# A selective scan on one core: 5 of 16 products with C moved to GpSimd and summed by accumulating DMAs

## The chip, the core and the metric

The kernel runs on one core of one Trainium2 chip. The metric is the device time of one execution, in microseconds (us); shown is the median of several runs. TensorE (PE), VectorE (DVE), ScalarE (ACT), GpSimd (POOL) and the DMA queue of SyncE (SP) work side by side; an instruction waits for semaphores that others set. Within an engine the instructions run in the order in which the program holds them.

## The reference, cut to what matters

Four layers follow one another on 4 images of 128 channels and 64 x 64 points: layer 0 is softmax attention over the 4096 points, layer 1 two 3x3 convolutions with quantised weights, layer 2 a Mamba block with group norm, layer 3 a second attention. The change is in layer 2. With 256 inner channels, 16 states per channel and a length of 4096 it computes

```python
def step(h, inp):
    dt_t, B_t, C_t, x_t = inp
    dA = jnp.exp(dt_t[..., None] * A)
    dBx = dt_t[..., None] * B_t[:, None, :] * x_t[..., None]
    h = dA * h + dBx
    y = jnp.einsum('bdn,bn->bd', h, C_t)
    return (h, y)
...
y = _selective_scan(xh, dt, Bmat, Cmat, A, D)
y = y * jax.nn.silu(z)
return y @ W_out
...
x = jax.nn.silu(_group_norm(x, gn_gamma, gn_beta))
return x + x_hsi
```

The sum over the 16 states in `y` (the einsum) is what the change distributes anew.

## The kernel before

Layer 2 of an image is cut into 8 groups of 512 points, so that there are 32 groups g. In each group the 16 states n are worked through one by one; m = 16 g + n counts these 512 steps. A tile of a step is 128 x 2 x 512 floats: both halves of the 256 channels, 512 points. One step takes

- a fetch on SP (`fetches`, L996): the rows B and C of state n, broadcast to 128 partitions (512 KB) into one of three tiles `bc`. It waits until the product with C of step m-3 is done, which is the last reader of that tile;
- on ACT two exponentials `da` into PSUM (`decays`, L1009);
- on DVE a multiplication `hs = ud * B` (`scans`, L1036), the product with C of the step before (`readout`, L1026, `hs = hs * C`), and two scans, one for each half (L1044). The first input of a scan, `da`, lies in PSUM, and the second, `hs`, in SBUF. The multiplications L1036 and L1026 have both inputs in SBUF;
- on ACT a copy of the last column of `hs` (`lasts`, L1019), from which the next group of the image goes on. It must be made before `hs` is overwritten by the product;
- on POOL an addition `y = y + hs` (`additions`, L1061).

After the 16th addition of a group POOL multiplies y by silu(z) (L1065, the gate), PE multiplies by W_out (L923), ACT writes the result to a tile `yo` of its own, and DVE takes the statistics of the group norm (L936). When an image's 8 tiles are there, the norm, silu (L972) and the residual (L976) are made in place, and the 8 tiles go to DRAM (L987). Layer 3 reads them from there (L375, tile `x_in`). There are three tiles `hs` and eight tiles `yo`.

Layers 0 and 3 of all images are worked through in 8 stages: (0,0), (0,1), (0,2), (3,0), (0,3), (3,1), (3,2), (3,3), given as layer and image. A stage computes blocks of energies on PE (L494), exponentials on ACT (L513) and weighted sums on PE (L556 for layer 0, L565 for layer 3), and runs beside the scans of some image. Stage (3,b) starts when layer 2 of image b is in DRAM.

The order of all instructions on all engines is made when the kernel is built: each piece of work is a Python generator that yields `op(engine, time, *needs)`, and `Order.run` (L79) takes the piece that could start earliest, by times written in the code and a rank. It treats the SBUF port that DVE and POOL share as one resource: each operation of POOL, and each of DVE that is marked `port=True`, has it to itself. The hardware then runs this order with waits on semaphores.

Of the kernel before, what the change touches and what calls it, by code (L numbers as in the profile page):

```python
# [8 lines left out]
F32 = mybir.dt.float32  # L9
# [7 lines left out]
ALU = mybir.AluOpType  # L17
# [24 lines left out]
VP = P + 1  # L42

# [90 lines left out]
def conv_seq_kernel(ctx: ExitStack, tc: tile.TileContext, i: dict, out: bass.AP):  # L134
# [226 lines left out]

    def stage_input(s):

        layer, b = stages[s]
        for c in range(NTB // 2):
            need = [("x2", b, 2 * c), ("x2", b, 2 * c + 1)] if layer == 3 else []
            need += [("sums", s * NS - 2 + c // 2), ("exp", s * NS - 1, 1)]
            yield op("SP", 0.1, *need, lag=3.5)
            x = att.tile([P, 2, 2, CB], F32, tag="p", name="x_in", bufs=4)
            x = x.rearrange("p a b c -> p a (b c)")  # L370
            if layer == 0:
                src = i["x"][b].rearrange("c (k r) w -> c k (r w)", r=ROWS)[:, 2 * c : 2 * c + 2]
            else:
                src = x2s[b][2 * c : 2 * c + 2].rearrange("c p t -> p c t")
            nc.sync.dma_start(out=x, in_=src)  # L375
            staged[s, c] = x
            mark("in", s, c)

    def operands(s):
# [19 lines left out]
        def high_low(o, g, key, bias, low, n):  # L399

            c = len(lows)
            lows.append(("low", s, c))
            yield op("ACT", 0.2 + n * 1e-3, (*key, "in"), *lows[c - 1 : c])
            h = att.tile([P, 2 * TB], F32R, tag="h", name="h", bufs=1)
            nc.scalar.activation(h[:, 0:n], g, AF.Identity, bias=low[1], scale=low[0])
            yield op("DVE", 0.06 + n * 1.2e-3)
            nc.vector.scalar_tensor_tensor(o, g, bias, h[:, 0:n], ALU.add, ALU.subtract)
            mark(*key)
            mark(*lows[c])
# [3 lines left out]
        for c in range(NTB // 2):  # L413
            g, key = yield from to_bank(1.9, ("in", s, c))
            if c == 0:
                its[s] = it = att.tile([P, N], dt, tag="it", name="it", bufs=1)
# [10 lines left out]
            need = [("sums", s * NS - 1)] if c == 0 and s else []  # L427
            g, key = yield from to_bank(1.1 if layer == 0 else 2.6, *need)
            if c == 0:
                v = att.tile([P, NJ * VP], F32, tag="v", name="v", bufs=1)  # L430
                if layer == 0:
                    vts[s] = v.rearrange("p (a b) -> p a b", b=VP)
                    nc.gpsimd.memset(vts[s][:, :, P:VP], 1.0)
                    jts[s] = att.tile([P, NJ // 2 * P], dt, tag="j", name="j", bufs=1)
                else:
                    both = v[:, 0 : NJ * P].rearrange("p (a b) -> p a b", a=2)
                    jts[s] = both[:, 0]
                    vts[s] = both[:, 1].rearrange("p (a b) -> p a b", b=D3)
# [83 lines left out]
    def accumulations():  # L522
        for t in filter(added, range(len(stages) * NS)):
            k, q = divmod(t, NQ)
            for h in range(2):
                if q == 0 and h == 0:
                    continue
                need = [("exp", t, h)]
                if q == 0 and k:
                    need.append(("sums", t - 1))  # L530
                yield op("DVE", 1.25, *need, port=True)
                if q == 0:
                    accs[k] = att.tile([P, 2, 2, CB], F32, tag="acc", name="acc", bufs=1)
                other = ps[t, 0] if q == 0 else accs[k]
                nc.vector.tensor_add(accs[k], ps[t, h], other)  # L535
# [248 lines left out]
    stats, live, bcs, das, hss = {}, {}, {}, {}, {}  # L784
# [129 lines left out]
    def output():  # L914
        for g in range(NG):
# [4 lines left out]
            yo = big.tile([P, TB], F32, tag="yo", name="yo", bufs=NTB)  # L920
# [15 lines left out]
            nc.vector.bn_stats(stats[b][:, c, :], yo)  # L936
            if c < NTB - 1:
                continue

# [29 lines left out]
            x2 = [live.pop(("yo", NTB * b + k)) for k in range(NTB)]  # L969
            for k in range(NTB):  # L970
                yield op("ACT", 0.69, table="silu")
                nc.scalar.activation(x2[k], x2[k], AF.Silu, bias=sh, scale=rs)  # L972
                mark("silu", b, k)
            for k in range(NTB):
                yield op("DVE", 0.75, port=True)
                nc.vector.scalar_tensor_tensor(  # L976
                    x2[k],
                    x1s[b % 2][:, 1 + k * TB : 1 + (k + 1) * TB],
                    1.0 / LEVELS,
                    x2[k],  # L980
                    ALU.mult,
                    ALU.add,
                )
                if k == 0:
                    x2s[b] = dram.tile([NTB, P, TB], F32, tag="x2", name="x2_d")
                yield op("SP", 0.1, lag=2.5)
                nc.sync.dma_start(out=x2s[b][k], in_=x2[k])  # L987
                mark("x2", b, k)
# [40 lines left out]
    def scans():  # L1029
        for m in range(NM):  # L1030
            g, n = divmod(m, DS)
            need = [("add", m - 3)] if m > 2 else []
            yield op("DVE", 1.25, ("bc", m), ("ud", g), *need, port=True)
            ud = live["in", g][1]
            hss[m] = hs = pair("hs", "hs", 3)
# [3 lines left out]
            if m:  # L1039
# [16 lines left out]
    def additions():  # L1056
        for m in range(NM):
            g, n = divmod(m, DS)
            yield op("POOL", 2.36, ("c", m), ("y", g))
# [3 lines left out]
            if n == DS - 1:  # L1063
                yield op("POOL", 2.4, ("sz", g))
# [503 lines left out]
```

## Time and profile before

| what | value |
|---|---|
| median of 3 runs | 3625.69 us (3621.45 to 3629.59) |
| profiled execution: its own time | 3621.05 us |
| its span | 3618.9 us |
| DVE busy | 3037.0 us, 84% of the span |
| PE busy | 3130.2 us, 86% |
| ACT busy | 2522.3 us, 70% |
| POOL busy | 1320.5 us, 36% |
| DMA queue of SP | 34.2% of 16 engines' span |

The profiler takes one execution. The page gives each engine's busy time, and groups of instructions by line with busy time, the mean length of one and the idle time before them. Other views are the timeline (instructions in order of time), sums by stretches of the span, and the waits. A first stretch up to 234 us has no scans, and from 3273 us on none is left: there only stage (3,3) runs.

### The profile page before, as it was taken

To read this page: it belongs to the slowest core of one execution; us is meant where nothing else is said; L and a number is where in the kernel's file an instruction comes from. 1 tells how busy PE (TensorE), PEld (TensorE's weight loads), DVE (VectorE), ACT (ScalarE), POOL (GpSimd) and SP (SyncE) were. 2 spreads that over 40 slices of the span, in tenths; PEclk is the share of its full clock that TensorE was granted. 3 is DMA by queue.
4 is the path that set the end of the run, shared out by engine and by line. 5 is a ranking of instruction groups with operands and counts; after the bars stand their busy time and mean duration, and the time that the engine had idled before them with its cause. 6 is when DMAs were issued, how large, how long until landed. Compare 5 with 4: busy or idle time off the path is not lost.

```text
span 3618.9 us, 69982 instructions
## 1 busy us (share of the span) xinstructions
PE 3130.2 (86%) x29495; PEld 2256.7 (62%) x29495; DVE 3037.0 (84%) x2872; ACT 2522.3 (70%) x3721; POOL 1320.5 (36%) x571
## 2 busy tenths in 40 slices
PE   5999899998999998999899999989779999205999
PEld 3988688886888755555787775555435555003665
DVE  2059999999999599999999999999999999994333
ACT  3477788787778777777787777777667776534444
POOL 0014344443444134444443344444444444451000
PEclk8999999999999999999999999999889999557999
DMA  2023433343434334444333333444354444341000
GB/s 72 1 58 93 107 96 89 96 100 103 98 93 100 88 96 106 111 108 129 90 98 106 79 105 95 107 107 106 101 139 108 109 110 106 94 105 62 13 19 17
DMA packets 203652, 327.76 MB, mean 91 GB/s; under 512 B 50608, under 2 KB 53440, under 8 KB 203328
## 3 DMA queue, kind: packets, MB, share of 16 engines
q1 hardware_dynamic: 196384, 322.09, 34.2%
q8 instruction: 233, 3.82, 0.4%
q10 hardware_dynamic: 6944, 1.10, 0.2%
q14 instruction: 91, 0.75, 0.1%
HBM read 304.27 MB, written 18.87 MB: 89 GB/s over the span
## 4 chain that ended last, share of the span: by engine, by line
PE 47%; DVE 33%; ACT 9%; issue 7%; DMA 3%; ACTq 0%; POOL 0%; SPq 0%; DVEq 0%; POOLq 0%
DVE hs L1044 14%; PE us L556 13%; PE e L494 11%; PE us L565 8%; DVE hs L1036 7%; DVE hs L1026 5%; PE us L589 3%; PE conv L704 2%; ACT p L513 2%; ACT da L1009 2%; PE yo L923 2%; PE xh L793 1%; PE proj L420 1%; DMA bc<-bc_d 1%; PE proj L462 1%
## 5 line engine op out<-in xcount | busy, mean ns | idle before, releaser
L1061 POOL TENSOR_TENSOR y<-y,hs 128x1024 f32<-128x1024 f32 x512 | 1218.2, 2379 | 1913.8 <-DVE hs L1026 1856.7
L513 ACT ACTIVATE p<-e 128x1024 f32<-128x1024 f32 x1024 | 1005.4, 1018 | 320.4 <-PE e L494 298.8
L1044 DVE TENSOR_TENSOR_SCAN hs<-da,hlast,hs 128x512 f32<-128x512 f32 x896 | 1099.9, 1264 | 16.1 <-ACT da L1009 15.9
L556 PE MATMUL us<-v,p 128*128 128x129 f32 x8192 | 1016.0, 281 | 47.4 <-ACT p L513 41.0
L556 PEld LDWEIGHTS us<-v,p 128*128 128x128 f32 x8192 | 960.4, 194 | 100.1 <-ACT p L513 45.2
L1009 ACT ACTIVATE da<-dt,amat 128x512 f32<-128x512 f32 x1024 | 702.5, 691 | 289.7 <-DVE hs L1044 284.7
L1026 DVE TENSOR_TENSOR hs<-hs,bc 128x1024 f32<-128x1024 f32 x512 | 666.9, 1303 | 15.2 <-ACT hlast L1019 14.6
L1036 DVE TENSOR_TENSOR hs<-ud,bc 128x1024 f32<-128x1024 f32 x512 | 653.0, 1275 | 1.0 <-DMA bc<-bc_d 0.6
L565 PE MATMUL us<-p,v 128*32 128x256 f32 x8192 | 525.0, 387 | 39.5 <-ACT p L513 37.2
L494 PE MATMUL e<-it,v 64*128 64x256 f32 x4096 | 528.2, 398 | 18.9 <-ACT p L513 17.9
L494 PEld LDWEIGHTS e<-it,v 64*128 64x128 f32 x4096 | 382.2, 191 | 168.9 <-issue 96.3
L565 PEld LDWEIGHTS us<-p,v 128*32 128x32 f32 x8192 | 238.1, 110 | 269.4 <-issue 86.0
L589 PE MATMUL us<-p,ones 128*32 128x256 f32 x3328 | 219.8, 382 | 0.0
L494 PE MATMUL e<-it,j 64*128 64x256 f32 x2048 | 196.0, 309 | 19.0 <-ACT v L396 9.9
L494 PEld LDWEIGHTS e<-it,j 64*128 64x128 f32 x2048 | 140.7, 189 | 77.8 <-issue 28.1
L793 PEld LDWEIGHTS <-w 128*128 128x128 bf16 x576 | 53.2, 99 | 192.9 <-issue 152.5
L1019 ACT COPY hlast<-hs 128x2 f32<-128x2 f32 x448 | 85.1, 190 | 120.0 <-DVE hs L1044 115.0
L589 PEld LDWEIGHTS us<-p,ones 128*32 128x32 f32 x3328 | 102.8, 110 | 87.9 <-issue 27.0
L793 PE MATMUL z<-x,w 128*128 128x512 fp8e4 x192 | 54.7, 395 | 117.4 <-ACT sz L816 112.4
L1044 DVE TENSOR_TENSOR_SCAN hs<-da,hs 128x512 f32<-128x512 f32 x128 | 149.4, 1203 | 1.4 <-ACT da L1009 1.3
L923 PE MATMUL yo<-y,w_out 128*128 128x512 f32 x128 | 67.6, 653 | 71.8 <-POOL y L1065 66.3
L535 DVE TENSOR_TENSOR acc<-p 128x1024 f32<-128x1024 f32 x16 | 19.6, 1225 | 126.8 <-PE us L589 99.2
(166 smaller groups left out, 2693.1 us busy)
## 6 DMA issues: line engine op xcount, KB each, us to landing
bc<-bc_d SPq DMA_DIRECT2D x512, 512.0 KB, 4.8
x_in<-in_x SPq DMA_DIRECT2D x16, 512.0 KB, 7.5
xpad<-in_x SPq DMA_DIRECT2D x32, 256.0 KB, 3.2
x_d<-yo SPq DMA_DIRECT2D x32, 256.0 KB, 2.4
x_in<-x_d SPq DMA_DIRECT2D x16, 512.0 KB, 7.1
o<-x_d SPq DMA_DIRECT2D x32, 256.0 KB, 5.4
out<-o SPq DMA_DIRECT2D x32, 256.0 KB, 2.2
bc_d<-xd SPq DMA_DIRECT2D x64, 32.0 KB, 1.9
```

Of the source, the lines that this page charges most:

```text
L494: nc.tensor.matmul(e[k % 4 // 2][:, k % 2, k // 4, :], lhsT=jts[s][row : row + D3, col : col + P], rhs=its[s][row : row + D3, c * CB : (c ...
L513: nc.scalar.activation(p, es[t][h], AF.Exp)
L556: nc.tensor.matmul(us[:, r, 0:VP], lhsT=ps[t, h][:, k % 2, k // 4, r * P : (r + 1) * P], rhs=vts[s][:, 8 * q + k, :], start=q == 0 and k = ...
L565: nc.tensor.matmul(us[m : m + 32, 0, :], lhsT=vts[s][:, 8 * q + k, m % D3 : m % D3 + 32], rhs=ps[t, h][:, k % 2, k // 4, :], start=q == 0 ...
L589: nc.tensor.matmul(us[32 * m : 32 * m + 32, 1, :], lhsT=ones[:, 0:32], rhs=term, start=False, stop=q == NQ - 1 and k >= len(terms) - 4,)
L793: nc.tensor.matmul(g, lhsT=w3[:, k // len(rhs), lhs[k % len(rhs)] : lhs[k % len(rhs)] + P], rhs=x[:, rhs[k % len(rhs)]], start=(k == 0), s ...
L923: nc.tensor.matmul(ps, lhsT=w_out[:, h, :], rhs=y[:, h, :], start=(h == 0), stop=(h == 1))
L1009: nc.scalar.activation(da, live["in", g][0][:, h, :], AF.Exp, scale=amat[:, h, n : n + 1])
L1026: nc.vector.tensor_mul(hs, hs, bcs.pop(m)[:, 1:2, :].to_broadcast([P, 2, TB]))
L1036: nc.vector.tensor_mul(hs, ud, bcs[m][:, 0:1, :].to_broadcast([P, 2, TB]))
L1044: nc.vector.tensor_tensor_scan(hs[:, h, :], das.pop((m, h)), hs[:, h, :], hlast[:, n, h : h + 1] if g % NTB else 0.0, ALU.mult, ALU.add,)
L1061: nc.gpsimd.tensor_tensor(y, y, hss.pop(m), ALU.add)
```

## The change

For the states n in `BY_DMA = (1, 4, 7, 10, 13)` the product with C is taken from DVE to POOL. For n = 1 POOL writes it to a new tile `y2`; for the other four it writes it in place into `hs`, and then issues a DMA from its own queue that adds `hs` to `y2` (`accum_op=ALU.add`). POOL's addition of `hs` to `y` falls away for these five. At the end of a group one more POOL instruction adds `y2` to `y`, ahead of the gate. `hs` has five tiles in place of three (`NHS`). `bc` keeps its three.

The space comes from four places. Only five tiles `yo` are kept; the first four of an image go to DRAM and come back after the norm's constants are known (`back`). The sum tile of the last stage shares the buffer of `j`. The tile `h` of the layer-0 projections is halved, and filled and used twice. A layer-3 stage reads its input chunks in the order 2, 3, 0, 1, so that the kept tiles come first.

```diff
+KEPT = 4
+BY_DMA = (1, 4, 7, 10, 13)
+NHS = 5
...
+    def halves_of(layer):
+        return range(NTB // 2) if layer == 0 else (2, 3, 0, 1)
...
-            yield op("ACT", 0.2 + n * 1e-3, (*key, "in"), *lows[c - 1 : c])
-            h = att.tile([P, 2 * TB], F32R, tag="h", name="h", bufs=1)
-            nc.scalar.activation(h[:, 0:n], g, AF.Identity, bias=low[1], scale=low[0])
-            yield op("DVE", 0.06 + n * 1.2e-3)
-            nc.vector.scalar_tensor_tensor(o, g, bias, h[:, 0:n], ALU.add, ALU.subtract)
+            for k in range(0, n, TB):
+                yield op("ACT", 0.71, *([(*key, "in"), *lows[c - 1 : c]] if k == 0 else []))
+                h = att.tile([P, TB], F32R, tag="h", name="h", bufs=1)
+                nc.scalar.activation(h, g[:, k : k + TB], AF.Identity, bias=low[1], scale=low[0])
+                yield op("DVE", 0.67)
+                nc.vector.scalar_tensor_tensor(
+                    o[:, k : k + TB], g[:, k : k + TB], bias, h, ALU.add, ALU.subtract
+                )
...
-                    accs[k] = att.tile([P, 2, 2, CB], F32, tag="acc", name="acc", bufs=1)
+                    accs[k] = att.tile([P, 2, 2, CB], F32, tag="j", name="acc", bufs=1)
...
-            yo = big.tile([P, TB], F32, tag="yo", name="yo", bufs=NTB)
+            yo = big.tile([P, TB], F32, tag="yo", name="yo", bufs=KEPT + 1)
...
+            if c < NTB - KEPT:
+                if c == 0:
+                    spilt[b] = dram.tile([NTB - KEPT, P, TB], F32, tag="yo", name="yo_d")
+                yield op("SP", 0.1, lag=2.5)
+                nc.sync.dma_start(out=spilt[b][c], in_=live.pop(("yo", g)))
+                mark("spilt", b, c)
...
+    def back(b):
+        for k in range(NTB - KEPT):
+            need = [("x2", b, NTB - KEPT + k - 1)] if k else []
+            yield op("SP", 0.1, ("spilt", b, k), *need, lag=3.0)
+            yo = big.tile([P, TB], F32, tag="yo", name="yo", bufs=KEPT + 1)
+            nc.sync.dma_start(out=yo, in_=spilt[b][k])
+            live["yo", NTB * b + k] = yo
+            mark("back", b, k)
...
-            need = [("add", m - 3)] if m > 2 else []
+            need = [("add", m - NHS)] if m >= NHS else []
             yield op("DVE", 1.25, ("bc", m), ("ud", g), *need, port=True)
             ud = live["in", g][1]
-            hss[m] = hs = pair("hs", "hs", 3)
+            hss[m] = hs = pair("hs", "hs", NHS)
             nc.vector.tensor_mul(hs, ud, bcs[m][:, 0:1, :].to_broadcast([P, 2, TB]))
             if n == 0:
                 mark("begun", g)
-            if m:
+            if m and (m - 1) % DS not in BY_DMA:
                 yield op("DVE", 1.22, ("last", m - 1), port=True)
                 readout(m - 1)
...
     def additions():
         for m in range(NM):
             g, n = divmod(m, DS)
+            if n in BY_DMA:
+                yield op("POOL", 2.36, ("s", m, 1), ("last", m))
+                hs = hss.pop(m)
+                if n == BY_DMA[0]:
+                    live["y2", g] = pair("y2", "y2", 1)
+                y2 = live["y2", g]
+                to = y2 if n == BY_DMA[0] else hs
+                c = bcs.pop(m)[:, 1:2, :].to_broadcast([P, 2, TB])
+                nc.gpsimd.tensor_tensor(to, hs, c, ALU.mult)
+                mark("c", m)
+                if n != BY_DMA[0]:
+                    yield op("POOL", 1.0, ("add", m - 3), lag=8.0)
+                    nc.gpsimd.dma_start(out=y2, in_=hs, accum_op=ALU.add)
+                mark("add", m)
+                continue
             yield op("POOL", 2.36, ("c", m), ("y", g))
             y = live["in", g][2]
             nc.gpsimd.tensor_tensor(y, y, hss.pop(m), ALU.add)
             mark("add", m)
             if n == DS - 1:
+                yield op("POOL", 2.36, ("add", g * DS + BY_DMA[-1]))
+                nc.gpsimd.tensor_tensor(y, y, live.pop(("y2", g)), ALU.add)
                 yield op("POOL", 2.4, ("sz", g))
                 nc.gpsimd.tensor_tensor(y, y, live.pop(("sz", g)), ALU.mult)
                 mark("gated", g)
```

More of the change, by code (lines that the diff above doesn't have):

```diff
@@ L360, in conv_seq_kernel @@
     its, jts, vts, es, ps, uss = {}, {}, {}, {}, {}, {}
+    def halves_of(layer):
+        return range(NTB // 2) if layer == 0 else (2, 3, 0, 1)
     def stage_input(s):
         layer, b = stages[s]
-        for c in range(NTB // 2):
+        for n, c in enumerate(halves_of(layer)):
             need = [("x2", b, 2 * c), ("x2", b, 2 * c + 1)] if layer == 3 else []
-            need += [("sums", s * NS - 2 + c // 2), ("exp", s * NS - 1, 1)]
+            need += [("sums", s * NS - 2 + n // 2), ("exp", s * NS - 1, 1)]
             yield op("SP", 0.1, *need, lag=3.5)
@@ L412, in operands @@
         it = None
-        for c in range(NTB // 2):
+        for n, c in enumerate(halves_of(layer)):
             g, key = yield from to_bank(1.9, ("in", s, c))
-            if c == 0:
+            if n == 0:
                 its[s] = it = att.tile([P, N], dt, tag="it", name="it", bufs=1)
@@ L426, in operands @@
                 order.add(4, copy(o, flat(g), key, 1.2))
-            need = [("sums", s * NS - 1)] if c == 0 and s else []
+            need = [("sums", s * NS - 1)] if n == 0 and s else []
             g, key = yield from to_bank(1.1 if layer == 0 else 2.6, *need)
-            if c == 0:
+            if n == 0:
                 v = att.tile([P, NJ * VP], F32, tag="v", name="v", bufs=1)
@@ L783, in conv_seq_kernel @@
     hlast = mam.tile([P, DS, 2], F32, tag="hlast", name="hlast")
-    stats, live, bcs, das, hss = {}, {}, {}, {}, {}
+    stats, live, bcs, das, hss, spilt = {}, {}, {}, {}, {}, {}
     def pair(name, tag, bufs):
@@ L936, in output @@
             nc.vector.bn_stats(stats[b][:, c, :], yo)
+            if c < NTB - KEPT:
[4 more added lines that the diff above has]
+                mark("spilt", b, c)
             if c < NTB - 1:
                 continue
+            order.add(2, back(b))
             yield op("DVE", 0.2)
@@ L968, in output @@
             nc.vector.tensor_sub(sh, gnb, sh)
[L969 to L988, printed above, removed]
+            x2s[b] = dram.tile([NTB, P, TB], F32, tag="x2", name="x2_d")
@@ new lines, in output @@
+            first = range(NTB - KEPT, NTB)
+            for ks in (first, *([k] for k in range(NTB - KEPT))):
+                for k in ks:
+                    need = [] if k in first else [("back", b, k)]
+                    yield op("ACT", 0.69, *need, table="silu")
+                    x2 = live["yo", NTB * b + k]
+                    nc.scalar.activation(x2, x2, AF.Silu, bias=sh, scale=rs)
+                for k in ks:
+                    x2 = live.pop(("yo", NTB * b + k))
+                    yield op("DVE", 0.75, port=True)
+                    nc.vector.scalar_tensor_tensor(
+                        x2,
+                        x1s[b % 2][:, 1 + k * TB : 1 + (k + 1) * TB],
+                        1.0 / LEVELS,
+                        x2,
+                        ALU.mult,
+                        ALU.add,
+                    )
+                    yield op("SP", 0.1, lag=2.5)
+                    nc.sync.dma_start(out=x2s[b][k], in_=x2)
+                    mark("x2", b, k)
```

## The prediction, made before the result was known

> **What bounds the kernel now.** I read the engine rows first. Nothing is idle enough to point at one engine, so I cut the span into stretches, by the stages of attention.
>
> ```profile
> PE 3130.2 (86%) x29495; PEld 2256.7 (62%) x29495; DVE 3037.0 (84%) x2872; ACT 2522.3 (70%) x3721; POOL 1320.5 (36%) x571
> ```
>
> ```profile
> core 0: us, PE busy (x) PEld busy (x) DVE busy (x) ACT busy (x) POOL busy (x), PEclk, DMA share, GB/s
> 240.00:1250.00 1010.00, 939.88 (x7312) 800.73 (x7311) 934.42 (x884) 791.76 (x1186) 407.20 (x170) 0.98 0.38 95
> 1250.00:2127.00 877.00, 812.88 (x7657) 585.34 (x7656) 838.52 (x780) 675.37 (x1017) 378.74 (x158) 0.97 0.39 104
> 2127.00:2640.00 513.00, 436.98 (x4648) 255.40 (x4646) 491.82 (x448) 377.92 (x564) 227.89 (x94) 0.93 0.41 108
> 2640.00:3060.00 420.00, 394.08 (x4452) 231.20 (x4456) 399.74 (x349) 314.84 (x483) 194.57 (x82) 0.98 0.45 112
> 3060.00:3290.00 230.00, 39.61 (x154) 17.41 (x146) 211.41 (x193) 99.44 (x157) 106.56 (x45) 0.54 0.36 92
> 3297.00:3619.00 322.00, 311.41 (x3713) 196.56 (x3713) 110.84 (x109) 144.03 (x169) 0.00 (x0) 0.98 0.07 22
> ```
>
> From 240 to 3060 us DVE (93 to 96% busy) and PE (85 to 94%) are both nearly full. From 3060 to 3290 PE is 17% busy: it has finished stage (3,2) and waits for the last scans, with DVE at 92%. Then stage (3,3) takes 322 us on PE alone. So the end of the scans, hence DVE's work, sets the end, and PE has some 190 us in hand. That is also the most that a faster DVE can bring before PE is late.
>
> Next, the rows of one step and the timeline of two.
>
> ```profile
> L1061 POOL TENSOR_TENSOR y<-y,hs 128x1024 f32<-128x1024 f32 x512 | 1218.2, 2379 | 1913.8 <-DVE hs L1026 1856.7
> L1026 DVE TENSOR_TENSOR hs<-hs,bc 128x1024 f32<-128x1024 f32 x512 | 666.9, 1303 | 15.2 <-ACT hlast L1019 14.6
> L1036 DVE TENSOR_TENSOR hs<-ud,bc 128x1024 f32<-128x1024 f32 x512 | 653.0, 1275 | 1.0 <-DMA bc<-bc_d 0.6
> ```
>
> ```profile
> 3160.64 1.28 DVE L1036 TENSOR_TENSOR hs<-ud,bc 128x1024 f32<-128x1024 f32 x1
> ...
> 3161.84 1.21 DVE L1026 TENSOR_TENSOR hs<-hs,bc 128x1024 f32<-128x1024 f32 x1
> 3162.97 2.44 DVE L1044 TENSOR_TENSOR_SCAN hs<-da,hlast,hs 128x512 f32<-128x512 f32 x2
> 3163.20 2.34 POOL L1061 TENSOR_TENSOR y<-y,hs 128x1024 f32<-128x1024 f32 x1 [2.36 <-DVE hs L1026]
> ```
>
> ```profile
> 3198.55 3.20 POOL L1065 TENSOR_TENSOR y<-y,sz 128x1024 f32<-128x1024 f32 x1
> 3199.48 3.35 DVE L1026 TENSOR_TENSOR hs<-hs,bc 128x1024 f32<-128x1024 f32 x1
> ```
>
> A step is 1.20 (multiplication) + 1.13 (product) + 2.37 (two scans) = 4.70 us, start to start. POOL's addition of 2.34 us lies under the scans, with 0.03 to spare. The last two lines show what happens when POOL has two instructions in a row, as at the end of a group: the gate waits for the running multiplication, takes the port at its end (3.20 = 0.85 of waiting + 2.35), and the product of n = 0 on DVE lasts 3.35 in place of 1.21. 21 of the 32 groups have this, at 2.17 us each, 45.5 us in all.
>
> **What the Trainium skill says.** "SBUF — State Buffer", Who interferes with whom: a DVE instruction with two SBUF inputs contends with a POOL instruction that reads SBUF, one waits for the other to end, and a DVE instruction with one SBUF input doesn't. The trace agrees, as above: scans (one input in PSUM) run beside POOL, products don't. "GPSIMD Engine Reference", 3.1: a two-input operation is 1.96 times as slow as on DVE; here 2.34 against 1.21, 1.93 times. "DMA: Bandwidth & Descriptors", SWDGE vs HWDGE: a DMA that accumulates can only be issued from POOL, whose cores write its descriptors. No such DMA is in the trace. The same page, Issuing engines are not separate DMA queues: all DMAs share the 16 engines. The trace agrees: a fetch of `bc` alone lands after 4.85 us (median), the one issued at 847 us beside two 512 KB loads after 6.70, the one at 2127 us after 6.27, and one beside a 256 KB load issued 0.4 us later after about 5.2.
>
> **The change, part by part**, in us, against the profiled 3621.05.
>
> Saved: 5 x 32 = 160 products leave DVE, each 1.13 start to start: -181. (By the row's mean of 1.303 it would be -208, but that mean holds the 45.5 us of blocking at n = 0, which isn't among the five states.)
>
> The product on POOL replaces an addition of the same shape. I take the same 2.35; one input is broadcast there, and DVE's L1026, also broadcast, is as fast as plain products. In a clean step it costs nothing: it waits for the copy of the last column (0.19 on ACT, just after the scan), by which time DVE is in the next multiplication, then takes the port and lies under the next scans. Without that cover each costs up to 2.35.
>
> (1) One more POOL instruction for each group, `y + y2`. I walk the group's end: addition 15 ends with the scans of the next group's n = 0; `y + y2` waits out a multiplication and blocks product 0, as the gate does now; the gate waits out product 0 and lies under scans 1; addition 0 lies under scans 2; product 1, long ready, comes behind it, waits out multiplication 3, and blocks product 2. So there are two blocks where there was one. With today's share of groups: 21 x 2.17 = +46 (bounds 0 and 32 x 2.17 = 69).
>
> (2) The late product 1 frees its `bc` tile late. From its end to the multiplication of state 4 DVE has product 2 and two scans, 1.13 + 2.37 = 3.5, and the fetch needs 4.85: 21 x 1.35 = +28 (bounds 0 and 43).
>
> (3) Products beside other DVE work. In the order of the built kernel 121 of the 160 are followed at once by the next multiplication. In 39 cases something else is between; in about 18 of them it doesn't need the port (statistics, a PSUM read, a clamp), so POOL starts at once and the next multiplication waits. I take 1.7 each: +31 (bounds 0 and 39 x 2.17 = 85).
>
> (4) The other fetches. Today a fetch has about 2.0 us to spare in plain steps, because product m-3 is early. Product m on POOL ends with the scans of m+1; then follow multiplication, product and scans, 4.77 us, until bc of m+3 is needed. From the built order, with these lengths, I took DVE's work in that interval for the states 4, 7, 10, 13: at least 4.77, median 5.84, a quarter over 7.79. Summed shortfalls: 3 us at 4.85 per fetch, 40 at 5.6, 66 at 6.0, 106 at 6.5, 150 at 7.0. The accumulating DMA of the same product starts just behind the fetch and moves 512 KB too, so the fetch stretches: estimated between the 5.2 and the 6.3 seen beside other loads, about 5.75: +50 (bounds 3 and 150).
>
> The issue of that DMA on POOL waits for the accumulate three states earlier (some 13 us back) and for POOL itself; behind it waits the next addition, which isn't ready until 2.3 us later, when DVE has done a multiplication and a product. Up to 2.3 us it costs nothing; each us more holds addition and port for 128 us in all. I take 0. A tile `hs` is wanted back after five steps, 16.5 us by the order; product (3.6) and accumulate (taken under 11) fit.
>
> (5) The tail: the last gate comes 2.4 us later. Four tiles that return from DRAM are the stage's last chunks; PE takes 4.7 us for each chunk, so they are there in time. The halved `h` adds a short instruction pair 16 times at stage starts, where PE waits: +5 for both. The 16 stores and 16 loads of spilling add 8 MB to 328 MB moved: nothing, but on SP they stand behind fetches that now wait longer.
>
> Sum: -181 + 46 + 28 + 31 + 50 + 5 = -21. 3621.05 - 21 = 3600; the median of the runs shown lies 4.64 above the profiled run: 3605.
>
> **The rivals.** *Most of the gain is kept*: DVE's own gaps between 250 and 3273 us are 162 us; what is new in (3) may fall into them, and the fetch may hardly stretch, since its packets leave over 3.6 us while the DMA engines are about 40% busy. Then -181 + 46 + 28 + 0 + 3 + 5 = -99: 3527. Against it: beside a load of half the size a fetch already takes 5.2. *Slower: the accumulates hold the fetches.* One mechanism: the 128 fetches issued with an accumulate take 6.7 us, as beside two loads at 847 us. Then (4) is 124, and half of the fetches behind ordinary products, whose slack falls short by 66 in sum at 6.7, are met too, +33: -181 + 46 + 28 + 31 + 124 + 33 + 5 = +86: 3712. It is slower from about 6.1 us per fetch on. For it: an accumulate reads two streams and writes one. *PE binds*: the order moves the scans only 2 to 9 steps further by each stage's start (stage (3,1) at step 318 for 314), so the first 2100 us might go at PE's pace, and the rest breaks even: 3626. Against it: the 190 us that PE has at the end.
>
> **How the numbers follow.** Small gain, 3605 (own range 3575 to 3650): 0.50, of it 0.29 faster, 0.10 same, 0.11 slower. Most kept, 3527: 0.20. Held fetches, 3712: 0.25. PE binds, 3626: 0.05, split over the three. A measurement can tell 0.2%, 7 us, from no change. The range from 3530 to 3710 leaves out half of each outer case.
>
> **What would show it.** Right: DVE's busy time falls by less than 181; products of n = 0 and n = 2 of about 3.4 us; POOL's products of 2.35 to 3.2; idle time ahead of the multiplication with the fetch of `bc` as its releaser, some 80 us in place of 0.6; fetches of 5.5 to 6. Wrong: products on POOL much longer than 2.4 when alone, an issue of the DMA that holds POOL over 2.3 us, DVE waiting for `hs` tiles, or PE full up to the end of the scans.

## The result and the profile after

The changed kernel takes 3776.06 us (median of 4 runs, 3774.22 to 3782.80), the kernel before 3625.96 beside it: a ratio of 1.042 (95% interval 1.040 to 1.0436). It is 150 us slower, where 21 us less were forecast. The profiled execution took 3782.8 us, its span is 3781.0, 162 us longer than before.

The engine rows of the changed kernel, and its sums by stretches (in each pair: busy us, number of instructions):

```profile
PE 3184.8 (84%) x29495; PEld 2282.8 (60%) x29495; DVE 2971.9 (79%) x2728; ACT 2540.4 (67%) x3748; POOL 1615.5 (43%) x731
```

```profile
core 0: us, PE busy (x) PEld busy (x) DVE busy (x) ACT busy (x) POOL busy (x), PEclk, DMA share, GB/s
239.00:1261.00 1022.00, 928.09 (x7003) 781.78 (x7001) 924.04 (x854) 782.32 (x1183) 494.79 (x219) 0.97 0.47 117
1261.00:2183.00 922.00, 828.00 (x7695) 594.92 (x7696) 799.92 (x711) 678.66 (x1014) 454.16 (x199) 0.96 0.48 120
2183.00:2700.00 517.00, 469.54 (x4936) 285.16 (x4934) 458.86 (x390) 367.65 (x551) 267.68 (x117) 0.96 0.48 121
2700.00:3160.00 460.00, 358.62 (x3756) 205.92 (x3760) 389.97 (x343) 318.39 (x484) 232.79 (x104) 0.89 0.53 129
3160.00:3440.00 280.00, 95.70 (x863) 49.44 (x855) 240.31 (x197) 131.59 (x205) 160.54 (x69) 0.65 0.48 117
3440.00:3781.00 341.00, 312.71 (x3717) 197.65 (x3717) 118.57 (x131) 151.47 (x179) 0.00 (x0) 0.95 0.09 29
```

DVE's busy time fell by 65 us and the kernel became longer. No engine is full any more: DVE is 85 to 90% busy in every stretch (92 to 96% before), PE 78 to 91% up to 3160 us. The end after the scans is nearly as before, so the loss lies in the scans' stretch. Its sums, before and after:

```profile
234.00:3273.00 3039.00, 2623.77 (x24239) 1891.67 (x24237) 2877.18 (x2639) 2260.31 (x3408) 1310.30 (x545) 0.94 0.39 102
```

```profile
239.00:3422.00 3183.00, 2676.06 (x24239) 1915.91 (x24237) 2807.22 (x2488) 2276.74 (x3431) 1600.62 (x703) 0.93 0.49 121
```

Length less busy time: DVE stood idle for 3039 - 2877 = 162 us before and for 3183 - 2807 = 376 after. These 214 us are more than the whole loss.

The rows that answer to those of before, and then the page's lines of the two DMAs (KB each, median us from issue to landing):

```profile
L1106 POOL TENSOR_TENSOR y<-y,hs 128x1024 f32<-128x1024 f32 x352 | 838.1, 2381 | 1510.3 <-DVE hs L1056 1498.6
...
L1066 DVE TENSOR_TENSOR hs<-ud,bc 128x1024 f32<-128x1024 f32 x512 | 714.8, 1396 | 25.5 <-DMA bc<-bc_d 22.7
...
L1056 DVE TENSOR_TENSOR hs<-hs,bc 128x1024 f32<-128x1024 f32 x352 | 481.6, 1368 | 15.4 <-ACT hlast L1049 15.2
L1097 POOL TENSOR_TENSOR hs<-hs,bc 128x1024 f32<-128x1024 f32 x128 | 364.3, 2846 | 215.6 <-ACT hlast L1049 204.1
```

```profile
bc<-bc_d SPq DMA_DIRECT2D x512, 512.0 KB, 5.1
y<-hs POOLq DMA_DIRECT2D x128, 512.0 KB, 7.5
```

The multiplication's mean rose from 1275 to 1396 ns, and ahead of it stand 22.7 us of waiting for `bc`. The timeline of a group's end, DVE first and then POOL, shows the forecast second block:

```profile
2395.93 1.32 DVE L1066 TENSOR_TENSOR hs<-ud,bc 128x1024 f32<-128x1024 f32 x1
2397.17 3.39 DVE L1056 TENSOR_TENSOR hs<-hs,bc 128x1024 f32<-128x1024 f32 x1
2400.48 2.44 DVE L1074 TENSOR_TENSOR_SCAN hs<-da,hlast,hs 128x512 f32<-128x512 f32 x2
2402.85 3.35 DVE L1066 TENSOR_TENSOR hs<-ud,bc 128x1024 f32<-128x1024 f32 x1
2406.30 2.46 DVE L1074 TENSOR_TENSOR_SCAN hs<-da,hlast,hs 128x512 f32<-128x512 f32 x2
```

```profile
2396.24 3.24 POOL L1110 TENSOR_TENSOR y<-y,y 128x1024 f32<-128x1024 f32 x1
2399.55 3.23 POOL L1112 TENSOR_TENSOR y<-y,sz 128x1024 f32<-128x1024 f32 x1
2402.72 2.39 POOL L1106 TENSOR_TENSOR y<-y,hs 128x1024 f32<-128x1024 f32 x1
2405.06 3.35 POOL L1097 TENSOR_TENSOR y<-hs,bc 128x1024 f32<-128x1024 f32 x1
```

`y + y2` (L1110) makes the product of n = 0 last 3.39 us. The addition of n = 0 (L1106) starts at 2402.72, right at the gate's end and 0.13 us ahead of the multiplication of n = 2, which therefore lasts 3.35. Only then comes the product of n = 1 on POOL, and waits for that multiplication to end (3.35 too). Of 20 long multiplications of n = 2 in this trace, 17 stand behind the addition and 3 behind the product. But the large loss is of another kind: DVE waits for results of PE and ACT. `rall` are the reciprocals of attention's sums, `xpad` is the output of layer 0, `q` belongs to layer 1, `stats` are the statistics of the group norm, and `yo` is the residual. DVE's waits before and after (total us, times, longest), one line for each place and the same places in both:

```profile
DVE rall L636 <- ACT us L617: 137.0, 18, 39.5
...
DVE xpad L647 <- PE ut L643: 20.5, 11, 4.3
DVE q L739 <- ACT q L736: 20.3, 8, 6.4
DVE hs L1044 <- ACT da L1009: 17.2, 12, 3.7
...
DVE stats L936 <- ACT yo L928: 13.1, 7, 9.4
...
DVE yo L976 <- ACT yo L972: 0.9, 1, 0.9
```

```profile
DVE rall L648 <- ACT us L629: 152.9, 21, 41.1
...
DVE stats L948 <- ACT yo L940: 89.6, 17, 11.8
...
DVE hs L1074 <- ACT da L1039: 43.8, 33, 4.4
DVE xpad L659 <- PE ut L655: 36.6, 11, 6.1
DVE q L751 <- ACT q L748: 34.7, 12, 7.2
...
DVE yo L999 <- ACT yo L995: 33.6, 11, 7.0
```

These grew by 14 to 77 us each; no wait of DVE's shrank by more than 8. One of the 17 waits ahead of the statistics, on all engines:

```profile
2422.14 1.98 PE L935 MATMUL yo<-y,w_out 128*128 128x512 f32 x4
...
2424.16 0.59 ACT L940 COPY yo<-yo 128x512 f32<-128x512 f32 x1 [0.78 <-PE yo L935]
2424.65 0.20 ACT L1049 COPY hlast<-hs 128x2 f32<-128x2 f32 x1
2424.78 0.69 DVE L948 BATCH_NORM_STATS2 stats<-yo 128x6 f32<-128x512 f32 x1 [6.36 <-ACT yo L940]
2424.92 2.37 POOL L1097 TENSOR_TENSOR hs<-hs,bc 128x1024 f32<-128x1024 f32 x1 [6.38 <-ACT hlast L1049]
...
2425.39 2.98 DVE L1066 TENSOR_TENSOR hs<-ud,bc 128x1024 f32<-128x1024 f32 x1
```

The gate (L1112) of this group ended at 2402.78, so POOL wasn't late: PE came to its projection 19 us later, and was busy for 16.8 of these with what stood ahead of it in its queue, mostly attention. In 16 of the 17 waits the gate had ended 9 us or more before the projection began. DVE stood before the statistics for 6.36 us, and the next multiplication stood behind them in its queue.

### The profile page after: what moved, and what is told of

Same layout as the page of the kernel before. It is cut to its first block, busy times and chain, and to the rows that moved or that the text cites. A ratio compares the mean times of both kernels' runs of the same rounds, so it can differ in the third digit from the quotient of the medians.

```text
span 3781.0 us, 70144 instructions
## 1 busy us (share of the span) xinstructions
PE 3184.8 (84%) x29495; PEld 2282.8 (60%) x29495; DVE 2971.9 (79%) x2728; ACT 2540.4 (67%) x3748; POOL 1615.5 (43%) x731
## 4 chain that ended last, share of the span: by engine, by line
PE 40%; DVE 33%; ACT 11%; issue 6%; DMA 6%; POOL 2%; SPq 0%; ACTq 0%; DVEq 0%; POOLq 0%
DVE hs L1074 13%; PE us L568 11%; PE e L506 10%; DVE hs L1066 8%; PE us L577 7%; DVE hs L1056 4%; DMA bc<-bc_d 3%; ACT da L1039 2%; ACT p L525 2%; PE us L601 2%; PE xh L805 2%; PE conv L716 1%; DVE ud L913 1%; POOL hs L1097 1%; PE proj L474 1%
## 5 line engine op out<-in xcount | busy, mean ns | idle before, releaser
L1106 POOL TENSOR_TENSOR y<-y,hs 128x1024 f32<-128x1024 f32 x352 | 838.1, 2381 | 1510.3 <-DVE hs L1056 1498.6
L568 PE MATMUL us<-v,p 128*128 128x129 f32 x8192 | 1032.2, 283 | 57.5 <-ACT p L525 40.7
L568 PEld LDWEIGHTS us<-v,p 128*128 128x128 f32 x8192 | 973.5, 196 | 117.1 <-ACT p L525 46.5
L1066 DVE TENSOR_TENSOR hs<-ud,bc 128x1024 f32<-128x1024 f32 x512 | 714.8, 1396 | 25.5 <-DMA bc<-bc_d 22.7
L506 PE MATMUL e<-it,v 64*128 64x256 f32 x4096 | 540.2, 403 | 34.5 <-ACT p L525 30.3
L1056 DVE TENSOR_TENSOR hs<-hs,bc 128x1024 f32<-128x1024 f32 x352 | 481.6, 1368 | 15.4 <-ACT hlast L1049 15.2
L1097 POOL TENSOR_TENSOR hs<-hs,bc 128x1024 f32<-128x1024 f32 x128 | 364.3, 2846 | 215.6 <-ACT hlast L1049 204.1
L1101 POOL DMA_DIRECT2D y<-hs x128 | 112.8, 881 | 41.0 <-POOL hs L1097 38.4
```

Source lines behind the costliest of these rows:

```text
L506: nc.tensor.matmul(e[k % 4 // 2][:, k % 2, k // 4, :], lhsT=jts[s][row : row + D3, col : col + P], rhs=its[s][row : row + D3, c * CB : (c ...
L568: nc.tensor.matmul(us[:, r, 0:VP], lhsT=ps[t, h][:, k % 2, k // 4, r * P : (r + 1) * P], rhs=vts[s][:, 8 * q + k, :], start=q == 0 and k = ...
L1056: nc.vector.tensor_mul(hs, hs, bcs.pop(m)[:, 1:2, :].to_broadcast([P, 2, TB]))
L1066: nc.vector.tensor_mul(hs, ud, bcs[m][:, 0:1, :].to_broadcast([P, 2, TB]))
L1097: nc.gpsimd.tensor_tensor(to, hs, c, ALU.mult)
L1106: nc.gpsimd.tensor_tensor(y, y, hss.pop(m), ALU.add)
```

## The experiments

My first theory was that POOL's detour costs the time, by a late gate above all (A). The rivals were the accumulates (B) and the room-making (C), later that freed DVE time is worth little (P against D), and that the order is what costs. A gain or loss in us is worked out below from the ratios, times 3628 us; between two of these ratios it is uncertain by some 8 to 10 us.

| kernel | us | ratio to before (95%) | DVE idle in the scans' stretch |
|---|---|---|---|
| before | 3626 to 3630 | 1 | 162 |
| changed | 3776 | 1.042 (1.040 to 1.0436) | 376 |
| e1 room only | 3665 | 1.010 (1.008 to 1.012) | 211 |
| e2 no accumulates | 3763 | 1.037 (1.035 to 1.039) | 358 |
| e3 no addition of y2 | 3736 | 1.029 (1.027 to 1.031) | 393 |
| e4 gate's lag in the plan | 3825 | 1.053 (1.051 to 1.055) | 447 |
| e5 products left out, new order | 3545 | 0.977 (0.9755 to 0.979) | 221 |
| e6 changed operations, order of e1 | 3704 | 1.021 (1.019 to 1.022) | 313 |
| e7 products left out, order of before | 3604 | 0.993 (0.992 to 0.995) | 271 |
| e8 before, gate's lag | 3682 | 1.015 (1.013 to 1.0165) | 220 |
| e9 before, less PE | 3601 | 0.992 (0.991 to 0.994) | 156 |
| e10 = e7 + e9 | 3559 | 0.9815 (0.980 to 0.983) | 240 |
| e11 changed, less PE | 3760 | 1.036 (1.035 to 1.038) | 359 |
| e12 changed, plan priced by the trace | 3860 | 1.065 (1.062 to 1.067) | 416 |
| e13 products on POOL, order of before | 3621 | 0.998 (0.997 to 0.999) | 258 |
| e14 changed, four bc, four hs | 3738 | 1.030 (1.028 to 1.031) | 339 |
| e15 spill only, new order | 3680 | 1.014 (1.012 to 1.015) | 224 |
| e16 = e6 without the sums | 3678 | 1.0125 (1.011 to 1.014) | 313 |
| e17 spill's traffic, order of before | 3630 | 0.9998 (0.999 to 1.001) | 171 |
| e18 before, plan priced by the trace | 3648 | 1.0055 (1.004 to 1.007) | 183 |

### The sums, in the changed kernel's own order (e2, e3)

```diff
 e2:
-                    nc.gpsimd.dma_start(out=y2, in_=hs, accum_op=ALU.add)
 e3:
                 yield op("POOL", 2.36, ("add", g * DS + BY_DMA[-1]))
-                nc.gpsimd.tensor_tensor(y, y, live.pop(("y2", g)), ALU.add)
+                live.pop(("y2", g))
```

> The changed kernel in the same order, without the 128 accumulating DMAs: four of five states are missing from y, their products on POOL are still made. Theory A: little moves, 3740 to 3776 us; the DVE waits for bc (23 us after the change) go, and POOL's 0.9 us per issue with it. Rival B (the accumulates take DMA bandwidth from fetches and everything else, and hold POOL): 3640 us or less, with the idle time of DVE in the scans' stretch down from 376 to below 250 us.

> The changed kernel in the same order, without the addition of y2 to y at a group's end, so five of the 16 states are missing from y; everything else, the accumulates too, is done. Theory A: the block of the multiplication of n = 2 (41 us) goes, the gate comes 3.2 us sooner, and of DVE's 78 us of waiting for the output tile ahead of the statistics about half goes: 3776 - 41 - 39 = some 3695 us, 3670 to 3720. If the group's end is not the place, only the block goes or even moves to the next instruction: 3735 to 3776.

Without the accumulates 18 us come back, of 150: rival B falls as the main cause. Without `y + y2` 46 come back, about the 41 us of blocks at n = 2. But the waits ahead of the statistics stay (90.7 us against 89.6), and this is against A: a gate that is some 3 us sooner does not shorten them.

### The gate's lag in the plan (e4, e8)

```diff
-                yield op("POOL", 2.4, ("sz", g))
+                yield op("POOL", 2.4, ("sz", g), lag=8.0)
```

> The changed kernel with one number altered: the planner is told that the gated y is usable 8 us later than POOL's instruction ends in its plan. All is computed; projection, copy of the output tile and statistics are thereby queued later on PE, ACT and DVE. If DVE's new idle time comes from waits of an in-order queue for a gate that is later on the chip than in the plan, the 78 us ahead of the statistics fall under 20 and part of the waits for da, q, us goes with them: 3680 to 3720 us. If those waits only stand in for POOL's or PE's pace, they turn up elsewhere: 3755 to 3790.

> The kernel before with one number altered, the 8 us of the gate's lag in the plan that made the changed kernel 49 us slower. All is computed, and no operation changes, only the order. If an order made anew costs some tens of us whatever it is for, because the one of before happens to suit the chip: 3660 us or more. If the lag was bad for the changed kernel alone: 3615 to 3640 us.

In e4 the wait ahead of the statistics did shrink, and another took its place; the changed kernel became 41 us slower:

```profile
DVE hs L1074 <- ACT da L1039: 126.0, 49, 7.4
...
DVE stats L948 <- ACT yo L940: 25.9, 13, 11.6
```

The scans' wait for `da` rose from 43.8 to 126.0 as that of the statistics fell from 89.6 to 25.9. So A fell: taking away the largest of the new waits did not shorten the kernel. And e8 shows that the kernel before, with every operation unchanged, loses 54 us by the same edit of the plan.

### The room-making (e1, e15, e17)

e1 is the changed kernel with `BY_DMA = ()` and without `y + y2`. e15 is the kernel before with the spill, `back` and the order 2, 3, 0, 1. e17 adds the traffic alone, where the order is fixed already (no `yield`):

```diff
...
             nc.vector.bn_stats(stats[b][:, c, :], yo)
+            if c < 4:
+                if c == 0:
+                    spilt[b] = dram.tile([4, P, TB], F32, tag="yo", name="yo_d")
+                nc.sync.dma_start(out=spilt[b][c], in_=yo)
             if c < NTB - 1:
                 continue
+            for k in range(4):
+                nc.sync.dma_start(out=live["yo", NTB * b + k], in_=spilt[b][k])
```

> Only the room-making part of the change: spilled output tiles, halved h, shared sum tile, the order 2, 3, 0, 1 and five hs tiles stay; all 16 products of a group are on DVE again and POOL adds all 16, so nothing is left out of the result. Theory A (the GpSimd detour loses the time: a second POOL instruction at each group's end, blocked DVE products and multiplications, a late gate behind which DVE's queue waits): 3625 to 3650 us, since only the tail's 19 us belong to this part, and DVE idle in the scans' stretch near the 162 us of before. Rival C (the spill and its place in SP's queue hold things up): 3690 us or more, with the residual waiting for silu some 20 us and the stage start waiting for x_in up to 37 us.

> The kernel before with the spill alone: five output tiles, four of an image go to DRAM and come back, layer 3 reads its input in the order 2, 3, 0, 1; h, the sum tile and three hs tiles as before. All is computed. The whole room-making part gave 3665 us. If the spill (residuals one by one behind loads, later input of the next stage) costs it: 3655 to 3670 us. If the halved h and the shared sum tile at stage starts and in the last stage cost it: 3630 to 3640 us.

> The kernel before, in its own order on PE, DVE, ACT and POOL, with the traffic of the spill: the first four output tiles of an image go to DRAM after their statistics, and come back into the same tiles (eight are kept) once the eighth has its statistics; silu waits for them. All is computed. If the spill's transfers cost its 52 us: 3660 us or more. If the new order costs it: 3625 to 3640 us.

e1 costs 36 us: 3665 lies between what A and C forecast. e15, a part of it, costs 50, more than either of its forecasts: costs of parts don't add up here. e17 costs nothing that can be measured. So in the old order the transfers are free, and what costs must come with the five tiles: the order made anew, or the residuals of a norm that go one by one in it. Which of these two weighs more wasn't tried.

### What DVE's freed time is worth (e5, e7, e13)

e5 takes the product out of the plan too; e7 and e13 keep each `yield` of before, so that all else stays in its place:

```diff
 e5:
-            if m:
+            if m and (m - 1) % DS not in FREE:
                 yield op("DVE", 1.22, ("last", m - 1), port=True)
 ...
 e7:
+        if m % DS not in FREE:
             nc.vector.tensor_mul(hs, hs, c)
 e13:
+        on = nc.gpsimd if m % DS in ON_POOL else nc.vector
+        on.tensor_tensor(hs, hs, c, ALU.mult)
 ...
-            nc.gpsimd.tensor_tensor(y, y, hss.pop(m), ALU.add)
+            hs = hss.pop(m)
+            if n not in ON_POOL:
+                nc.gpsimd.tensor_tensor(y, y, hs, ALU.add)
```

> The kernel before, with the products with C of the states 1, 4, 7, 10, 13 left out altogether (the raw state is added to y instead, so the result is another one): DVE is freed of the same 160 products at no price, nothing moves to POOL, no DMA is added, and the planner orders everything anew. Theory D (DVE's work sets the end, as the prediction had it): 3627 - 181 = 3446 us, up to 3480. Theory P (most of the way the scans go at the pace that PE and the fixed order give, so that DVE's time saved turns into DVE waiting): 3560 us or more, with DVE idle in the scans' stretch at 250 us or more in place of 162.

> The kernel before with the same 160 products left out (the raw state is added to y, so the result is another one), but in the order of before on every engine: nothing is planned anew. Theory D: about 3446 us, as DVE works off the same queue faster. Theory P: 3560 us or more; DVE's busy time falls by 193 us, and its waits for PE and ACT grow by more than half of that.

> The kernel before, in its own order, with the products of states 1, 4, 7, 10, 13 made on POOL in place of POOL's additions of these states, which are left out (they are missing from y). No room is made, no accumulate, no y2, three hs tiles. It differs from the kernel with the products left out in the same order (3604 us) by the products' later end alone. If the product on POOL is nearly free: 3600 to 3620 us. If late products hold bc, hs and the port: 3640 us or more, with DVE waiting for bc or hs ahead of the multiplications of n = 4, 7, 10, 13 and 0.

This decides. 160 products that vanish, with nothing in their place, bring 24 us in the old order, not 181. The engine row of e7, and the sums of its scans' stretch:

```profile
PE 3133.9 (87%) x29495; PEld 2259.1 (63%) x29495; DVE 2910.1 (81%) x2712; ACT 2511.7 (70%) x3721; POOL 1437.6 (40%) x571
```

```profile
235.00:3257.00 3022.00, 2627.58 (x24239) 1894.11 (x24238) 2750.90 (x2479) 2249.70 (x3408) 1427.36 (x545) 0.93 0.38 103
```

DVE is busy for 127 us less than before (3037.0 to 2910.1), since POOL's additions block other instructions more often (the subtraction on `ud` grew by 16 us, the multiplications by 15), and it is idle for 271 us in place of 162: of the 126 us less in the stretch, 109 turned into waiting. Where it waits:

```profile
DVE rall L638 <- ACT us L619: 148.9, 25, 39.5
...
DVE rall L674 <- PE sc L665: 53.1, 20, 6.0
DVE hs L1030 <- ACT hlast L1021: 35.6, 40, 3.4
DVE hs L1048 <- ACT da L1011: 30.0, 24, 3.0
DVE xpad L649 <- PE ut L645: 28.0, 18, 4.3
```

These are results of attention, and the scans' own loop through ACT (`hlast` 35.6 where it was 14.6, `da` 30.0 where it was 17.2), each by 8 to 25 us. In e5 the order was made for the lighter DVE; it brings 83 us, still less than half, and with 3545 us and 221 us of idle time lies between D and P. So the same operations gain 59 us by this order made anew (e5 against e7). e13 puts the products on POOL at 16 us over their absence, with DVE's waits for `bc` at 5.2 us in sum: of the 24 us that the freed time is worth in this order, the move takes 16.

### Less PE (e9, e10, e11)

```diff
-                    if k % 4 // 2 != h:
+                    if k % 4 // 2 != h or (k == 3 and s < 7):
                         continue
```

> The kernel before, in its own order, with one in eight of the attention's weighted-sum matmuls on PE left out in all stages but the last (about 127 us of layer 0's and 49 us of layer 3's; those terms are missing from the sums). PE is freed of some 176 us beside the scans, nothing else is touched. If PE paces the scans' stretch: 3628 - 176 = 3450 to 3510 us. If neither PE nor DVE paces it alone, and the fixed order makes each wait for the other: 3570 to 3610 us, like the 24 us that the freed DVE gave in the same order. If DVE paces it: 3615 to 3630 us.

> Both reliefs at once, in the order of before: the 160 products with C left out on DVE and one in eight of the weighted-sum matmuls on PE (both parts of the result are altered). If the engines wait for each other, the two together bring more than the sum of the two alone: 3480 us or less where the sum of the two single gains would be some 60 us. If a third thing paces (ACT, the latency from engine to engine), the two together bring no more than their sum.

> The changed kernel in its own order with the same matmuls left out on PE (those terms are missing from the sums). If the changed kernel is slow because its order makes DVE wait for PE (DVE waits for output tiles, sums and projections that PE is late with), it gains more than the kernel before does from the same relief: 3776 - 120 = some 3650 us or less, with the 78 us of waiting ahead of the statistics under 40. If it is slow for POOL's sake, it gains no more than the kernel before does.

The relief was smaller than I had put it. The engine row of e9 shows PE 82 us less busy than before, not 176:

```profile
PE 3048.0 (85%) x27703; PEld 2164.5 (60%) x27703; DVE 3036.6 (84%) x2872; ACT 2517.9 (70%) x3721; POOL 1319.6 (37%) x571
```

It brings 28 us, and 11 of these before the first multiplication of the scans, which starts at 223 us in place of 234. DVE's relief brings 24, both together 67. That is 15 more than their sum, uncertain by some 10, and far from the leap that two engines in lockstep alone would give. The changed kernel gains some 20, not more than the kernel before, and its waits ahead of the statistics stay at 84.4 us. So PE's amount of work is not what makes it slower than the kernel before.

### The changed operations in other orders (e6, e16, e14, e12, e18)

In e6 DVE's order is that of e1, without the five products: the `yield` of each is kept, and the instruction issued there goes to POOL; the accumulate is issued where POOL's addition stood, and `y + y2` right ahead of the gate. e16 leaves out the accumulates and `y + y2`.

```diff
 e6, readout(m):
+        if n not in BY_DMA:
+            nc.vector.tensor_mul(hs, hs, c)
+        elif n == BY_DMA[0]:
+            live["y2", g] = y2 = pair("y2", "y2", 1)
+            nc.gpsimd.tensor_tensor(y2, hs, c, ALU.mult)
+        else:
+            nc.gpsimd.tensor_tensor(hs, hs, c, ALU.mult)
 ...
 e14:
-NHS = 5
+NHS = 4
 ...
-            need = [("c", m - 3)] if m > 2 else []
+            need = [("c", m - 4)] if m > 3 else []
 ...
-            bcs[m] = bc = mam.tile([P, 2, TB], F32, tag="bc", name="bc", bufs=3)
+            bcs[m] = bc = mam.tile([P, 2, TB], F32, tag="bc", name="bc", bufs=4)
 e12:
-                yield op("POOL", 2.36, ("s", m, 1), ("last", m))
+                yield op("POOL", 2.85, ("s", m, 1), ("last", m))
 ...
-                    yield op("POOL", 1.0, ("add", m - 3), lag=8.0)
+                    yield op("POOL", 0.88, ("add", m - 3), lag=7.5)
 e18:
-            yield op("DVE", 1.25, ("bc", m), ("ud", g), *need, port=True)
+            yield op("DVE", 1.20, ("bc", m), ("ud", g), *need, port=True)
 ...
-                yield op("DVE", 1.22, ("last", m - 1), port=True)
+                yield op("DVE", 1.13, ("last", m - 1), port=True)
 ...
-                yield op("DVE", 1.26, ("da", m, h))
+                yield op("DVE", 1.19, ("da", m, h))
```

> The changed kernel's operations (five products on POOL, accumulates, the addition of y2) in the order that the planner makes for the room-only kernel, whose products are all on DVE: DVE's order is that kernel's, without the 160 products. All is computed. If the new order is to blame (operations fine, the planner's arrangement bad): 3664 - 181 + the blocks (46 and 31) + 20 for bc = some 3580 us. If the operations are to blame, or DVE's time is worth nothing there: 3740 us or more.

> The changed operations in the room-only kernel's order (3704 us with all of them), without the accumulates and without the addition of y2: five states are missing from y, their products on POOL are made. If the sums' share is what it was in the changed kernel's own order (14 for the accumulates, 40 for the addition of y2): 3650 us, and the five products on POOL then bring a gain of some 15 us against the room-only kernel's 3665. If the products on POOL cost the most: 3680 us or more.

> The changed kernel with four tiles bc and four tiles hs in place of three and five; all is computed, ordered anew. If the late release of bc by POOL is what spoils the changed kernel's order and pace: 3690 us or less, no waits for bc. If it is just another order: 3700 to 3860 us, as the others; if hs tiles then run out, DVE waits for the accumulates ahead of multiplications.

> The changed kernel with three numbers of the planner set to what its own trace shows: the product on POOL 2.85 in place of 2.36, the issue 0.88 in place of 1.0, its landing 7.5 in place of 8.0 us. All is computed, and only the order changes. If the changed kernel lost because its plan had wrong prices: 3700 us or less. If an order made anew is worth some tens of us either way, whatever it was made for: anything from 3700 to 3830 us, as with the 3704 and 3825 us of two other orders of the same operations.

> The kernel before with three numbers of the planner set to what the trace shows, start to start: the multiplication 1.20 in place of 1.25, the product 1.13 in place of 1.22, a scan 1.19 in place of 1.26. All is computed, only the order changes. If the order of before suits the chip by its particular prices, and any other costs some tens of us: 3650 to 3690 us. If prices nearer to the chip make a better order: 3600 us or less, which would beat both kernels.

The order alone moves the same operations: the changed ones took 3704, 3776, 3825 and 3860 us in four orders, those of before 3628, 3648 and 3682 in three. The changed kernel's own order is 77 us worse than e6's, whose 3704 lies between its two forecasts. Plans nearer to the trace's durations gave no better order, neither for the changed kernel (e12, 83 us slower, beyond its forecast range) nor for the one before (e18, 20 slower). e14 is 44 us faster than the changed kernel and has no wait for `bc`, where that one had 22.7; as the order changed too, the rest can't be assigned. In e6's order the products cost 9 us against e1, hardly more than the uncertainty, where a gain of 15 was one forecast, and the sums 30. None of the kernels that compute all beats the one before.

## Why the prediction was wrong, step by step

**The step that failed** is the first term of the sum, "Saved: 5 x 32 = 160 products leave DVE, each 1.13 start to start: -181", with the sentence that it rests on: "the end of the scans, hence DVE's work, sets the end, and PE has some 190 us in hand". It took each us off DVE as a us off the end. The runs show 24 us in a fixed order (e7) and 83 in a new one (e5), for the same 160 products left out. PE's 190 us lie after its last stage but one; up to 2127 us, where most of the scans run, PE was 93% busy in the same view, and I had read that line without using it. The fault isn't PE's pace alone (e9, e11). In e7, 109 of the 126 us by which DVE had less to do became idle time: its waits for ACT grew by 64 us and those for PE by 33. I read this as in-order queues that hand results to each other all the time, where an engine that gets ahead waits at the next hand-over. The waits fit it, but no run isolates it, and none relieves ACT.

**A term was missing**: the order made anew. The prediction took from it only where the blocks fall and how far the scans are at each stage's start. The 152 us between the kernels, taken one step at a time, are: room with its order 36 (e1), products on POOL in that order 9, the freed time included (e16), sums 30 (e6), the changed kernel's own order 77. The split holds for this path; by another the parts are others, as e2 and e3 show for the sums (18 and 46).

**Right in size, and but for one step in mechanism.** (1) Two blocks at the group's end: products of n = 0 took 53.5 us of excess in place of 45.5, multiplications of n = 2 41 in place of 3: +47, forecast +46. The walk missed its last step: the second block is made by addition 0, not by product 1, and hits the multiplication of n = 2, not the product. (3) Multiplications of n = 5, 8, 11, 14: +29, forecast +31. The issue of the accumulate, 0.88 us, costs nothing that DVE's waits show, and DVE waits for an `hs` tile for 1.2 us in all. The spill's transfers cost nothing in the old order (e17). (5) From the last product to the span's end 354 us, 345 before: +9, forecast +5.

**Mis-sized.** (2) and (4): 28 and 50 us of waits for `bc` were forecast, and 22.7 came, 3.7 of them at n = 4. For (4), fetches landed after 5.1 us (median), not 5.75. For (2), product 1 ends at 2408.41 in the timeline above, with the scans of n = 2, and so ahead of the multiplication of n = 3 and not behind it; that leaves its fetch some 1.2 us more. Not foreseen: blocks of the subtraction on `ud` (L913), 18 us, and of the multiplication of n = 1, 7 us.

With the measured terms in place of mine the sum would be -181 + 47 + 29 + 18 + 7 + 22 + 9 = -49. The span grew by 162. Of the 211 between, 192 are DVE's further waits (376 - 162 - 22); the rest is the later start of the scans (239 us in place of 234) and other busy time of DVE.

**The rivals.** Held fetches came nearest in time (3712), by the wrong mechanism: the accumulates cost 18 us, and the fetches behind a product on POOL took 5.1 to 5.3 us (medians for n = 7, 10, 13 and 0), not 6.7. The accumulates did stretch fetches one state later: medians of 5.92 us at n = 1 and 6.17 at n = 11, against 4.97 and 4.93 in e2. These had slack: no multiplication of these two states waited for its `bc`. "PE binds" had the doubt about DVE's freed time, but not the loss. What I called a sign of being wrong, POOL's products above 2.4 us alone, an issue above 2.3, waits for `hs` tiles, PE full up to the end of the scans, didn't occur (`hs` but for 1.2 us); the list had no sign for DVE waiting on PE and ACT, and that is what came.

One rival has no experiment of its own: the clock granted to PE, 0.93 in the scans' stretch after and 0.94 before, with PE busy for 2676 and 2624 us on the same 24239 matmuls. An order can lose without it: e8 loses 54 us, and PE is busy for 3126 us in all, 4 less than before. And the drops to half clock come behind idle time of PE: in the 3.4 us ahead of the changed kernel's 49 drops in this stretch PE was 35% busy on average, 84% over the whole stretch. What the lower clock adds to the loss is open.

**What stays open**: what makes one order better than another. For the operations of before the new orders lost 20 and 54 us, for less work one won 59 (e5), and the changed operations did best, by 77 us, in an order made for another kernel (e6). Among the kernels that compute all, DVE's idle time goes roughly with the time. That is little more than bookkeeping, since what the stretch doesn't spend on DVE's work is idle time of DVE, and it is no rule for a good order. That the order of before beats the two others tried for it is shown; why is not.

## What to carry to other kernels

Where an order fixed at build time keeps two engines above 90%, a us taken off one of them is not a us off the end: leave the work out without any replacement and measure what its absence is worth, before building anything that moves it. Do it in the same order and in one made anew; here this gave 24 and 83 us of 181. An order made anew has an effect of its own, of either sign: here it lost 20 and 54 us on unchanged operations, and gained 59 with the products left out. So measure the planned edit with the old order held, and the new order with the old operations. Slack at the end of a profile is not slack along the way: read each stretch for itself.

## What the runs showed of the hardware

- A DMA of 512 KB that adds into SBUF held POOL for 0.88 us at its issue and landed after 7.5 us (4.5 to 11.0). Without its 128 accumulates (e2) the median fetch took 4.9 us in place of 5.1, and the kernel 18 us less.
- In the timeline at 2396 us a POOL instruction that waits for the port gets it at the end of the running DVE instruction, ahead of DVE's next one, and a chain of both alternates: 3.24 and 3.23 us on POOL, 3.39 on DVE between them. A POOL instruction that starts 0.13 us ahead of a multiplication holds it up just so (3.35).
- A scan right behind its own multiplication starts 0.10 us after that one's recorded end (2406.20 to 2406.30), while the product behind a multiplication, which doesn't need its result, starts 0.08 before it.
- 1792 matmuls fewer on PE, about 176 us by their share of their rows' busy time, made it only 82 us less busy (e9).
